# Narrow matmul groups for layer 2's values and scores, a new place for its values in the time slot, and small VectorE instructions rewritten or moved to ScalarE

## The chip, the cores and the metric

The kernel runs on one core of a Trainium2 chip. The metric is the device time of one execution in microseconds (us), which is slightly longer than the span that the profile covers. The core's engines work in parallel, each through its own list of instructions in a fixed order: TensorE (PE, with its weight loads shown apart as PEld), VectorE (DVE), ScalarE (ACT), GpSimd (POOL) and SyncE (SP, which here issues every transfer). They wait for each other by semaphores. Matmul results land in PSUM and are carried from there to SBUF by DVE or ACT.

## What is computed

Four attention layers follow each other on x (4 images of 1024 rows and 256 columns). Layers 0 and 1 fill the first 1713 us and are touched only in one side job. Layer 2 is cross attention of 16 heads of width 16 to a context of 77 rows, with a factor for each score and a mask:

```python
scores = jnp.einsum('bhqd,bhkd->bhqk', q, k) / jnp.sqrt(jnp.float32(d))
scores = scores * attention_weights
scores = jnp.where(attention_mask, -jnp.inf, scores)
p_attn = jax.nn.softmax(scores, axis=-1)
out = jnp.einsum('bhqk,bhkd->bhqd', p_attn, v)
...
x = queries + out          # after out @ Wo.T + bo
return (x - mu) * jax.lax.rsqrt(var + LN_EPS) * gamma + beta
```

Layer 3 is a cross attention of 16 heads of width 64 to the same 77 context rows, after an RMS norm. All is float32.

## The kernel before

**Stages.** Layers 0 and 1 run over image and group of four heads, with a planner (`step`, `Job`) that puts side jobs between bursts of score matmuls. A side job has a share of the step in which its pieces are due; `values2` (layer 2's values of the context) and `keys2` are such jobs in layer 0. The values go to DRAM tensors and come back when layer 2 begins.

**Layers 2 and 3** run in time slots, one per tile of 128 rows (32 tiles, i = 0 to 31). `slot23` writes the order of the work in a slot by hand. A tile's layer 2 is spread over six slots: scores (`score2`) and maxima in slot i, exponentials (`exps2`), sums (`sums_of`, tile `den2`) and division (`divided`, POOL) in i+1, transposition (`turned_into`, tile `pT2`) in i+3, values (`values_of2`) in i+4, output (`out2`, `add2`) in i+5. Layer 3 of a tile starts 12 slots later (`LAG`): scores and their exponential (`score3`, `exp3`), in the next slot sums and division, in the one after it transposition (`pT3`) and output (`out3`). So slots 0 to 11 hold layer 2 alone, 12 to 36 both, 37 to 45 layer 3 alone. A middle slot has one tile of each stage. On PE its order is: transposition for layer 3, `score2`, `out3`, `values_of2`, `score3`, transposition for layer 2, `out2`.

**Between the layers** `between(g)` works on four tiles at a time: mean and variance (`stats4` on DVE, the power on POOL, L293), normalising on ACT (L1502), gamma and beta on POOL, statistics again, scaling by the inverse RMS (`normed`, L316, tile `xn`, four instructions on DVE), and transposition into `xT3` (`turned_x`, two DVE instructions, L1442). Its pieces are taken up at the four calls of `more()` in a slot, two pieces a call. `prep2(b)` (the queries of an image) is taken up in the same way, in two slots of an image.

**PSUM.** Pair tiles of two banks (`big`, 2 buffers) hold scores; the pool `sm` has 3 buffers that every transposition, `pvT` and projection takes in turn, so each new one waits until the third before it has been read out; the pool `pv` has one, for `po2` and `po3`.

**Scores of layer 2 before.** The keys stand in `kb` four times, each time with only every fourth head's rows kept. A matmul takes 64 rows (4 heads) and 4 x 77 columns; there are two such per pair tile and two pair tiles. Every float32 matmul other than a transposition shows as two instructions in the profile.

**Values of layer 2 before.** The 1232 columns (16 heads x 77) of the transposed weights fill 10 chunks of 128 rows. The values stand in DRAM as a block diagonal matrix, 128 output columns wide, loaded with five transfers per image (`loads2`), and `values_of2` multiplies chunk by chunk: 11 matmuls of 128 x 128 on 128 columns.

**Maxima.** L1558 bounds the 16 maxima of each row and scales them, in one DVE instruction on 128 x 16.

Of the kernel before, what the change touches and what calls it, by code (L numbers as in the profile page):

```python
# [31 lines left out]
def tile_xattn_seq(ctx: ExitStack, tc: tile.TileContext, d: dict, out: bass.AP):  # L32
# [902 lines left out]
    HALF, DIAG = HH * S * P, S * P + DH  # L935
    kept_v = dram.tile([NB, 2, HH * DIAG], F32, name="kept_v")
    stg = wpool.tile([P, 1024], F32, name="stg", tag="s7")
    turn = [0]

# [25 lines left out]

    def values2():

        n = NB * 2 * HH * DIAG // P // 8
        nc.gpsimd.memset(stg[:, 0:n], 0.0)
        nc.sync.dma_start(  # L970
            out=kept_v.rearrange("b e x -> (b e x)").rearrange("(p k n) -> p k n", p=P, n=n),
            in_=stg[:, 0:n].unsqueeze(1).to_broadcast([P, 8, n]),
        )
        yield
        for b in range(NB):
            pk = sm.tile([S, D], F32, name="pk", tag="sm")
            for c in range(2):
                mm(pk, ctxT[:, b, c, :], l2["Wv"][:, c, :], start=(c == 0), stop=(c == 1))
            v = place(3, NS)[:S, 0:D]
            nc.vector.tensor_tensor(v, pk, rows["bv2"][:S], ALU.add)  # L980
            for e in range(2):
                to = kept_v[b, e].rearrange("(j x) -> j x", x=DIAG)[:, 0 : S * P]
                nc.sync.dma_start(
                    out=to.rearrange("j (s p) -> s j p", p=P)[:, :, 0:DH],
                    in_=v[:, P * e : P * e + P].rearrange("s (j r) -> s j r", r=DH),
                )
            yield

    def keys2():
# [419 lines left out]

    def loads2(b):  # L1410

        V = late.tile([P, NC + 1, P], F32, name="V2", tag="V2", bufs=2)
        lo, hi = [kept_v[b, e, 0:HALF].rearrange("(r n) -> r n", n=P) for e in range(2)]

        k = HH * S % P
        nc.gpsimd.memset(V[:, 4:6, :], 0.0)
        nc.sync.dma_start(
            out=V[:, 0:4, :], in_=lo[0 : 4 * P].rearrange("(c p) n -> p c n", p=P)
        )
        nc.sync.dma_start(out=V[0:k, 4, :], in_=lo[4 * P :])  # L1420
        nc.sync.dma_start(out=V[k:P, 5, :], in_=hi[0 : P - k])
        nc.sync.dma_start(
            out=V[:, 6:10, :], in_=hi[P - k : 5 * P - k].rearrange("(c p) n -> p c n", p=P)
        )
        nc.sync.dma_start(out=V[0:HSIZE, 10, :], in_=hi[5 * P - k :])
        shared["v2", b] = V
        yield

    def half_rows(e):
        return slice(64 * e, 64 * e + 64)  # L1430

    def turned_x(dst, rows, g):

        for c in range(2):
            pt = sm.tile([P, 4, P], F32, name="ptx", tag="sm")
            for i in range(4):
                nc.tensor.transpose(pt[:, i, :], rows[i][:, c * P : (c + 1) * P], ident)
            src = pt.rearrange("p i n -> p (i n)")
            if g is None:
                nc.scalar.copy(dst[:, c, :], src)  # L1440
            else:
                nc.vector.tensor_scalar(dst[:, c, :], src, g[:, c : c + 1], None, ALU.mult)  # L1442
            yield

    def prep2(b):
# [42 lines left out]
    def between(g):  # L1488

        b, t0 = divmod(4 * g, NT)  # L1490
        x = xs[b]
        st = small.tile([P, 4, 6], F32, name="st4", tag="st6")
        mv = small.tile([P, 4, 2], F32, name="mv4", tag="mv", bufs=3)
        rs = small.tile([P, 4], F32, name="rs4", tag="rs", bufs=3)
        yield from stats4(st, mv, rs, g, 1e-5, False)
        away = late.tile([P, 4], F32, name="away", tag="away")
        nc.gpsimd.tensor_tensor(away, mv[:, :, 0], rs, ALU.mult)
        nc.gpsimd.tensor_scalar(away, away, -1.0, None, ALU.mult)
        yield True
        for k in range(4):  # L1500
            xt = x[:, t0 + k, :]
            nc.scalar.activation(  # L1502
                xt, xt, AF.Identity, bias=away[:, k : k + 1], scale=rs[:, k : k + 1]
            )
            nc.gpsimd.tensor_tensor(xt, xt, rows["gamma"], ALU.mult)
            nc.gpsimd.tensor_tensor(xt, xt, rows["beta"], ALU.add)
            yield k == 3
        st = small.tile([P, 4, 6], F32, name="st4", tag="st6")
        mv = small.tile([P, 4, 2], F32, name="mv4", tag="mv", bufs=3)
        rs = small.tile([P, 4], F32, name="rs4", tag="rs", bufs=3)  # L1510
        yield from stats4(st, mv, rs, g, 1e-6, True)
        xn = []
        for k in range(4):
            xt = small.tile([P, D], F32, name="xn", tag="xn", bufs=4)
            normed(xt, x[:, t0 + k, :], None, rs, k)
            xn.append(xt)
            if k % 2:
                yield k == 3
        yield True
        xT = shared["xT3"][:, g % 2]  # L1520
        yield from turned_x(xT, xn, cols["L3_xattn_norm_w"])
        shared["ready3"] = g

    LAG = 12

    def score2(a, i):

        b, t = a["b"], a["t"]
        qT, kb = shared["b2", b], shared["k2"]
        assert shared["ready2"] >= b  # L1530
        fs, mk = shared.pop(("side", i))
        if i + 1 < NB * NT:
            load_sides(i + 1)
        s = a["s"] = new_scores("s2", 4)
        for o in range(2):
            ps = pair_tile()
            for e in range(2):
                r = half_rows(e)
                mm(
                    ps[:, e, 0 : 4 * S].rearrange("p (h s) -> p h s", s=S),  # L1540
                    qT[r, o, P * t : P * t + P],
                    kb[r, o, :, b, :],
                )
            so = slice(o * HH * S, (o + 1) * HH * S)
            nc.vector.tensor_tensor(
                s[:, so].rearrange("p (i n) -> p i n", i=2), ps[:, :, 0 : 4 * S],
                fs[:, so].rearrange("p (i n) -> p i n", i=2), ALU.mult,
            )
        sv = s[:, 0:HK]
        nc.vector.copy_predicated(sv, mk, low.to_broadcast([P, HK]))  # L1550

    def maxima2(a):
        nm = a["nm"] = late.tile([P, H], F32, name="nm", tag="m16")
        nc.vector.tensor_reduce(
            nm, a["s"][:, 0:HK].rearrange("p (h k) -> p h k", k=S), axis=AX.X, op=ALU.max
        )

        nc.vector.tensor_scalar(nm, nm, 0.1 * NEG, -SC, ALU.max, ALU.mult)  # L1558

    def exps2(a, heads):  # L1560
        for h in heads:
# [22 lines left out]
    def values_of2(a):  # L1584

        V = shared["v2", a["b"]]
        pv = sm.tile([P, 2, P], F32, name="pvT", tag="sm")
        for k in range(NC + 1):
            o, c = (0, k) if k < 5 else (1, k - 1)
            r = slice(0, rows_in(c))  # L1590
            mm(pv[:, o, :], V[r, k, :], a["pT"][r, c, :], start=k in (0, 5), stop=k in (4, NC))
        oT = a["oT"] = late.tile([P, 2, P], F32, name="oT", tag="oT", bufs=2)
        nc.scalar.copy(oT, pv)

# [50 lines left out]
    def slot23(i, two, three, more):  # L1645
# [29 lines left out]
        elif i < n + 5:  # L1675
# [9 lines left out]
            if p1:  # L1685
                exps2(p1, range(4, 8))
            more()
            if c2:
                out3(c2)
            if p1:  # L1690
                exps2(p1, range(8, 12))
            if a:
                maxima2(a)
            if p4:
                values_of2(p4)
            more()
            if p1:
                exps2(p1, range(12, H))
            if c:
                score3(c, j)  # L1700
            more()
            if p3:
                turned_into(p3, "pT2")
            if c:
                exp3(c)
            if p1:
                sums_of(p1, "den2")
            if p5:
                out2(p5)
                add2(p5)  # L1710
            more()
            if p1:
                divided(p1)
# [36 lines left out]
    def jobs0(b, quad):  # L1750
# [142 lines left out]
    late = ctx.enter_context(tc.tile_pool(name="late", bufs=2))  # L1893
    kb = shared["k2"] = late.tile([P, 2, 4, NB, S], F32, name="kb", tag="kb", bufs=1)
    nc.sync.dma_start(out=kb.rearrange("p o h b s -> p o h (b s)"), in_=kept_k)
    load_sides(0)
    run(loads2(0))
    run(prep2(0))
# [65 lines left out]
```

## Time and profile before

| | us |
|---|---|
| median of 3 runs (2308.59 to 2311.46) | 2310.94 |
| the profiled execution, whole | 2310.56 |
| its span in the profile | 2308.8 |
| PE busy / DVE busy / ACT busy / POOL busy | 2158.3 / 1506.8 / 1027.5 / 652.2 |
| first load of layer 2's stage issued | 1713.2 |
| last layer 2 score tile masked (slot 31) | 2140.8 |

The span is 1.76 us shorter than the execution's time, and that execution is 0.38 us faster than the median. Busy shares over the whole span mix four layers, so everything that follows is read from the window of 1713 to 2309 us. PE's "busy" counts a matmul from its start to a modelled end; starts of consecutive matmul groups show better where PE was held up.

### The profile page before, as it was taken

To read this page: it belongs to the slowest core of one execution; us is meant where nothing else is said; L and a number is where in the kernel's file an instruction comes from. 1 tells how busy PE (TensorE), PEld (TensorE's weight loads), DVE (VectorE), ACT (ScalarE), POOL (GpSimd) and SP (SyncE) were. 2 spreads that over 40 slices of the span, in tenths; PEclk is the share of its full clock that TensorE was granted. 3 is DMA by queue.
4 is the path that set the end of the run, shared out by engine and by line. 5 is a ranking of instruction groups with operands and counts; after the bars stand their busy time and mean duration, and the time that the engine had idled before them with its cause. 6 is when DMAs were issued, how large, how long until landed. Compare 5 with 4: busy or idle time off the path is not lost.

```text
span 2308.8 us, 41140 instructions
## 1 busy us (share of the span) xinstructions
PE 2158.3 (93%) x16842; PEld 1358.9 (59%) x16874; DVE 1506.8 (65%) x2476; ACT 1027.5 (45%) x1716; POOL 652.2 (28%) x959
## 2 busy tenths in 40 slices
PE   4999999999999999999989999999988899999999
PEld 2544444555555455554556665666656678788877
DVE  3756567755566455754375666777748888788654
ACT  1144444434444444344533444544547655555322
POOL 2011113111131112310152233333333444444432
PEclk9899999999999999999989999999999999999999
DMA  7221121100000000101000010111025412313000
GB/s 217 55 57 68 31 65 41 40 6 15 7 15 2 10 11 6 38 1 19 6 15 6 15 26 16 21 20 20 15 74 152 136 51 68 100 49 95 10 10 17
DMA packets 87858, 93.98 MB, mean 41 GB/s; under 512 B 35714, under 2 KB 77558, under 8 KB 87542
## 3 DMA queue, kind: packets, MB, share of 16 engines
q1 hardware_dynamic: 87670, 91.35, 15.2%
q8 instruction: 133, 2.18, 0.4%
q14 instruction: 55, 0.45, 0.1%
HBM read 55.31 MB, written 18.39 MB: 32 GB/s over the span
## 4 chain that ended last, share of the span: by engine, by line
PE 67%; DVE 15%; ACT 4%; issue 2%; POOL 2%; DMA 0%; DVEq 0%; ACTq 0%; POOLq 0%; SPq 0%
PE ps L51 26%; PE po L51 12%; PE pv L51 6%; PE pp L51 5%; PE ph L51 4%; DVE mpart L672 3%; PE pvT L51 2%; DVE ms L1138 2%; PE ppv L51 2%; PE psT L1375 2%; PE pvw L51 1%; DVE mrow L1142 1%; PE pm L590 1%; PE pt L607 1%; ACT pe L738 1%
## 5 line engine op out<-in xcount | busy, mean ns | idle before, releaser
L51 PE MATMUL ps<-qk 32*128 32x192 f32 (+9 forms) x6528 | 581.8, 428 | 57.9 <-DVE mpart L672 25.1
L738 ACT ACTIVATE pe<-ps 128x1024 f32<-128x1024 f32 (+2 forms) x384 | 363.3, 952 | 589.5 <-PE ps L51 579.9
L51 PEld LDWEIGHTS ps<-qk 32*128 32x128 f32 (+1 forms) x6528 | 315.8, 185 | 295.6 <-issue 75.3
L672 DVE TENSOR_REDUCE mpart<-ps 128x2 f32<-128x1024 f32 (+4 forms) x384 | 331.0, 885 | 241.6 <-PE ps L51 240.8
L741 POOL TENSOR_SCALAR_AFFINE_SELECT pe<-pe 128x256 f32<-128x256 f32 (+1 forms) x192 | 95.2, 497 | 665.3 <-ACT pe L738 664.3
L1214 ACT ACTIVATE pew<-ps 128x768 f32<-128x768 f32 x128 | 103.4, 812 | 196.4 <-PE ps L51 196.4
L1574 POOL TENSOR_TENSOR s<-s,den 128x1232 f32<-128x1232 f32 x64 | 144.2, 2254 | 130.2 <-DVE den L1570 125.2
L1219 POOL TENSOR_SCALAR_AFFINE_SELECT pew<-pew 128x512 f32<-128x512 f32 x128 | 81.9, 640 | 337.7 <-ACT pew L1214 337.6
L1138 DVE TENSOR_TENSOR ms<-ps,maskw 128x768 f32<-128x768 f32 x128 | 122.1, 954 | 69.6 <-PE ps L51 68.1
L51 PE MATMUL po<-U,pT 128*128 128x256 f32 (+1 forms) x640 | 147.2, 385 | 10.8 <-DVE x L1602 7.6
L51 PE MATMUL pv<-pe,va 128*32 128x512 f32 (+3 forms) x1536 | 157.1, 496 | 0.0
L51 PE MATMUL ph<-yT,w 128*128 128x256 f32 x512 | 143.1, 401 | 2.4 <-DVE va L401 1.0
L51 PEld LDWEIGHTS po<-U,pT 128*128 128x128 f32 (+1 forms) x640 | 120.3, 192 | 35.0 <-ACT pT L1376 19.6
L51 PEld LDWEIGHTS po<-w,hT 128*128 128x128 f32 x800 | 111.8, 193 | 47.7 <-issue 38.9
L51 PE MATMUL ps<-G,xT 128*128 128x308 f32 x512 | 139.2, 422 | 0.0
L51 PE MATMUL po<-w,hT 128*128 128x128 f32 (+1 forms) x800 | 138.1, 317 | 0.9 <-ACT hT L904 0.9
L1563 ACT ACTIVATE s<-s,nm 128x77 f32<-128x77 f32 x512 | 134.8, 358 | 5.9 <-DVE nm L1558 5.9
L1376 ACT COPY pT<-psT 128x512 f32<-128x512 f32 (+1 forms) x192 | 87.7, 522 | 105.8 <-PE psT L1375 105.2
L665 DVE TENSOR_REDUCE mpart<-ps 128x8 f32<-128x1024 f32 x64 | 78.2, 1225 | 82.6 <-PE ps L51 80.0
L51 PEld LDWEIGHTS ph<-yT,w 128*128 128x128 f32 x512 | 88.8, 192 | 64.0 <-issue 50.8
L1142 DVE TENSOR_REDUCE mrow<-ms 128x4 f32<-128x768 f32 x128 | 122.2, 955 | 4.4
L51 PEld LDWEIGHTS ps<-G,xT 128*128 128x128 f32 x512 | 94.3, 190 | 30.1
(202 smaller groups left out, 3297.6 us busy)
## 6 DMA issues: line engine op xcount, KB each, us to landing
side<-in_fside_t SPq DMA_DIRECT2D x32, 616.0 KB
qk<-st SPq DMA_DIRECT2D x256, 64.0 KB
side<-in_mask_t SPq DMA_DIRECT2D x32, 154.0 KB
G<-kept_g SPq DMA_DIRECT2D x4, 1232.0 KB
U<-kept_u SPq DMA_DIRECT2D x4, 1152.0 KB
x<-in_x SPq DMA_DIRECT2D x8, 512.0 KB
out<-x SPq DMA_DIRECT2D x32, 128.0 KB
kept_g<-st SPq DMA_DIRECT2D x22, 154.0 KB
```

What stands on the lines that cost most here:

```text
L51: nc.tensor.matmul(o, lhsT, rhs, start=start, stop=stop, **kw)
L665: nc.vector.tensor_reduce(mpart[self.own][:, :, 2 * p : 2 * p + 2, 0].rearrange("p t j -> p j t"), ps.rearrange("p j (t n) -> p j t n", n= ...
L672: nc.vector.tensor_reduce(mpart[bl][:, i, 2 * p : 2 * p + 2, ci], ps[:, :, o : o + w], axis=AX.X, op=ALU.max,)
L738: nc.scalar.activation(pp[:n, :, o:512], ps[:n, :, o:512], AF.Exp, scale=SC)
L741: nc.gpsimd.affine_select(out=own, in_=own, compare_op=ALU.is_ge, fill=0.0, base=0, pattern=[[0, 2], [0, k], [1, P]], channel_multiplier=-1,)
L1138: nc.vector.tensor_tensor(v, ps.rearrange("p j (i n) -> p j i n", i=2)[:, :, :, 0:n], (maskw[:, 1:2] if w else maskw).unsqueeze(1).to_broa ...
L1142: nc.vector.tensor_reduce(mo, v, axis=AX.X, op=ALU.max, negate=True)
L1214: nc.scalar.activation(pp[:, :, :, 0 : P + WIN], ps.rearrange("p j (i n) -> p j i n", i=2)[:, :, :, 0 : P + WIN], AF.Exp, scale=SC,)
L1219: nc.gpsimd.affine_select(out=pf[:, :, 0:P], in_=pf[:, :, 0:P], compare_op=ALU.is_ge, fill=0.0, base=0, pattern=[[0, 4], [1, P]], channel_ ...
L1376: nc.scalar.copy(pT[:, 4 * group : 4 * group + n, :], ps[:, 0:n, :])
L1563: nc.scalar.activation(hs, hs, AF.Exp, bias=a["nm"][:, h : h + 1], scale=SC)
L1574: nc.gpsimd.tensor_tensor(s3, s3, a["den"].unsqueeze(2).to_broadcast([P, H, S]), ALU.mult)
```

## The change

*Values.* They are written to a DRAM tensor `kept_w` in rows of 32 (a pair of heads, each in its half of the row). A new side job `spread2`, taken up in layer 0 while image 2 is worked on, copies them from DRAM to DRAM into `kept_v`, with 17 transfers: `CUTS` holds the 17 pieces into which 8 head pairs (154 rows each) and 10 chunks of 128 rows cut each other. An image's values then come with one transfer. `values_of2` has 17 matmuls with 128 x 32 weights; the four head pairs of a half write 32 output rows each, in turn.

*Scores.* `score2` has 8 matmuls, each with 32 rows (2 heads) and 2 x 77 columns. The four row groups write to four PSUM banks, so both pair tiles are filled before the first is read out, and each of the two DVE instructions that reads them (L1545 before) takes half of the columns of both halves.

*Small instructions.* L1558 becomes two `tensor_tensor` with a tile `bound` of two columns; `xn` and `xT3` are made by ACT.

*Order.* In a slot of both layers `values_of2` comes before `out3`, and `out2` and `add2` before the transposition for layer 2.

```diff
+    PAIR = 2 * S
+    CUTS = [
+        (c, q, max(P * c, PAIR * q), min(P * c + P, PAIR * q + PAIR))
+        for q in range(HH) for c in range(PAIR * q // P, (PAIR * q + PAIR - 1) // P + 1)
+    ]
+    kept_w = dram.tile([NB, HK, HP], F32, name="kept_w")
+    kept_v = dram.tile([NB, P, len(CUTS), HP], F32, name="kept_v")
...
+    def spread2():
+        for k, (c, q, lo, hi) in enumerate(CUTS):
+            nc.sync.dma_start(
+                out=kept_v[:, lo - P * c : hi - P * c, k, :], in_=kept_w[:, lo:hi, :]
+            )
+            yield
...
-        V = late.tile([P, NC + 1, P], F32, name="V2", tag="V2", bufs=2)
...
+        V = late.tile([P, len(CUTS), HP], F32, name="V2", tag="V2", bufs=2)
+        nc.sync.dma_start(out=V, in_=kept_v[b])
...
-                nc.vector.tensor_scalar(dst[:, c, :], src, g[:, c : c + 1], None, ALU.mult)
+                nc.scalar.activation(dst[:, c, :], src, AF.Copy, scale=g[:, c : c + 1])
...
-            normed(xt, x[:, t0 + k, :], None, rs, k)
+            nc.scalar.activation(xt, x[:, t0 + k, :], AF.Copy, scale=rs[:, k : k + 1])
...
+        pair = [pair_tile() for _ in range(2)]
         for o in range(2):
-            ps = pair_tile()
-            for e in range(2):
-                r = half_rows(e)
+            for g in range(4):
+                e = 2 * (g % 2)
                 mm(
...
+                    qT[rows_of(g), o, P * t : P * t + P], kb[rows_of(g), o, e : e + 2, b, :],
+                    skip_group_check=True,
                 )
...
-        nc.vector.tensor_scalar(nm, nm, 0.1 * NEG, -SC, ALU.max, ALU.mult)
+        nc.vector.tensor_tensor(nm, nm, bound[:, 0:1].to_broadcast([P, H]), ALU.max)
+        nc.vector.tensor_tensor(nm, nm, bound[:, 1:2].to_broadcast([P, H]), ALU.mult)
...
-        for k in range(NC + 1):
-            o, c = (0, k) if k < 5 else (1, k - 1)
-            r = slice(0, rows_in(c))
-            mm(pv[:, o, :], V[r, k, :], a["pT"][r, c, :], start=k in (0, 5), stop=k in (4, NC))
+        for o in range(2):
+            own = [
+                [(k, c) for k, (c, q, _, _) in enumerate(CUTS) if q == 4 * o + j] for j in range(4)
+            ]
+            for n in range(max(map(len, own))):
+                for j in range(4):
+                    if n < len(own[j]):
+                        k, c = own[j][n]
+                        mm(
+                            pv[rows_of(j), o, :], V[:, k, :], a["pT"][:, c, :],
+                            start=(n == 0), stop=(n == len(own[j]) - 1), skip_group_check=True,
+                        )
...
             more()
+            if p4:
+                values_of2(p4)
             if c2:
                 out3(c2)
...
             if a:
                 maxima2(a)
-            if p4:
-                values_of2(p4)
             more()
...
             if c:
                 score3(c, j)
             more()
+            if p5:
+                out2(p5)
+                add2(p5)
             if p3:
                 turned_into(p3, "pT2")
...
-            if p5:
-                out2(p5)
-                add2(p5)
             more()
...
+        if b == 2:
+            j.append(Job(keep("sp2", spread2), 5, 0.3, 0.9))
```

More of the change, by code (lines that the diff above doesn't have):

```diff
@@ L933, in tile_xattn_seq @@
     kept_u = dram.tile([NB, H, S, D], F32, name="kept_u")
-    HALF, DIAG = HH * S * P, S * P + DH
-    kept_v = dram.tile([NB, 2, HH * DIAG], F32, name="kept_v")
+    PAIR = 2 * S
[5 more added lines that the diff above has]
+    kept_v = dram.tile([NB, P, len(CUTS), HP], F32, name="kept_v")
     stg = wpool.tile([P, 1024], F32, name="stg", tag="s7")
@@ L966, in values2 @@
     def values2():
-        n = NB * 2 * HH * DIAG // P // 8
+        n = len(CUTS) * HP
         nc.gpsimd.memset(stg[:, 0:n], 0.0)
         nc.sync.dma_start(
-            out=kept_v.rearrange("b e x -> (b e x)").rearrange("(p k n) -> p k n", p=P, n=n),
-            in_=stg[:, 0:n].unsqueeze(1).to_broadcast([P, 8, n]),
+            out=kept_v.rearrange("b p k n -> p b (k n)"),
+            in_=stg[:, 0:n].unsqueeze(1).to_broadcast([P, NB, n]),
+        )
+        nc.sync.dma_start(
+            out=kept_w.rearrange("b (s q) n -> s b (q n)", s=S),
+            in_=stg[:S, 0 : H * HP].unsqueeze(1).to_broadcast([S, NB, H * HP]),
         )
@@ L981, in values2 @@
             for e in range(2):
-                to = kept_v[b, e].rearrange("(j x) -> j x", x=DIAG)[:, 0 : S * P]
                 nc.sync.dma_start(
-                    out=to.rearrange("j (s p) -> s j p", p=P)[:, :, 0:DH],
-                    in_=v[:, P * e : P * e + P].rearrange("s (j r) -> s j r", r=DH),
-                )
+                    out=kept_w[b].rearrange("(q e s) n -> e s q n", e=2, s=S)[e, :, :, DH * e : DH * e + DH],
+                    in_=v.rearrange("s (q e r) -> s q e r", e=2, r=DH)[:, :, e, :],
+                )
+            yield
+    def spread2():
+        for k, (c, q, lo, hi) in enumerate(CUTS):
+            nc.sync.dma_start(
+                out=kept_v[:, lo - P * c : hi - P * c, k, :], in_=kept_w[:, lo:hi, :]
+            )
             yield
@@ L1410, in loads2 @@
     def loads2(b):
-        V = late.tile([P, NC + 1, P], F32, name="V2", tag="V2", bufs=2)
[L1413 to L1425, printed above, removed]
+        V = late.tile([P, len(CUTS), HP], F32, name="V2", tag="V2", bufs=2)
+        nc.sync.dma_start(out=V, in_=kept_v[b])
         shared["v2", b] = V
@@ L1534, in score2, with of_pair @@
         s = a["s"] = new_scores("s2", 4)
+        pair = [pair_tile() for _ in range(2)]
         for o in range(2):
-            ps = pair_tile()
-            for e in range(2):
-                r = half_rows(e)
-                mm(
-                    ps[:, e, 0 : 4 * S].rearrange("p (h s) -> p h s", s=S),
-                    qT[r, o, P * t : P * t + P],
-                    kb[r, o, :, b, :],
-                )
-            so = slice(o * HH * S, (o + 1) * HH * S)
+            for g in range(4):
+                e = 2 * (g % 2)
+                mm(
+                    pair[g // 2][:, g % 2, PAIR * o : PAIR * o + PAIR].rearrange(
+                        "p (h s) -> p h s", s=S
+                    ),
+                    qT[rows_of(g), o, P * t : P * t + P], kb[rows_of(g), o, e : e + 2, b, :],
+                    skip_group_check=True,
+                )
+        def of_pair(v, k):
+            v = v[:, 0:HK].rearrange("p (o g n) -> p g o n", o=2, g=4)
+            return v[:, 2 * k : 2 * k + 2]
+        for k in range(2):
             nc.vector.tensor_tensor(
-                s[:, so].rearrange("p (i n) -> p i n", i=2), ps[:, :, 0 : 4 * S],
-                fs[:, so].rearrange("p (i n) -> p i n", i=2), ALU.mult,
+                of_pair(s, k),
+                pair[k][:, :, 0 : 2 * PAIR].rearrange("p i (o n) -> p i o n", o=2),
+                of_pair(fs, k), ALU.mult,
             )
@@ L1587, in values_of2 @@
         pv = sm.tile([P, 2, P], F32, name="pvT", tag="sm")
-        for k in range(NC + 1):
-            o, c = (0, k) if k < 5 else (1, k - 1)
-            r = slice(0, rows_in(c))
-            mm(pv[:, o, :], V[r, k, :], a["pT"][r, c, :], start=k in (0, 5), stop=k in (4, NC))
+        for o in range(2):
[9 more added lines that the diff above has]
+                            start=(n == 0), stop=(n == len(own[j]) - 1), skip_group_check=True,
+                        )
         oT = a["oT"] = late.tile([P, 2, P], F32, name="oT", tag="oT", bufs=2)
@@ L1895, in tile_xattn_seq @@
     nc.sync.dma_start(out=kb.rearrange("p o h b s -> p o h (b s)"), in_=kept_k)
+    bound = late.tile([P, 2], F32, name="bound", tag="bound", bufs=1)
+    nc.gpsimd.memset(bound[:, 0:1], 0.1 * NEG)
+    nc.gpsimd.memset(bound[:, 1:2], -SC)
     load_sides(0)
```

## The prediction

> **What bounds the kernel now.** The page's busy shares say PE (93%), but over four layers. I read windows of the last stage first: PE, PEld, DVE, ACT and POOL busy, with counts, then the granted clock and the DMA share.
>
> ```profile
> 1770.00:1800.00 30.00, 27.14 (x190) 21.54 (x188) 26.16 (x38) 24.22 (x82) 11.19 (x11) 1.00 0.44 145
> 1900.00:1950.00 50.00, 49.28 (x294) 41.20 (x294) 45.49 (x69) 27.00 (x79) 25.20 (x31) 1.00 0.15 46
> 2200.00:2250.00 50.00, 47.24 (x234) 38.27 (x233) 28.21 (x53) 13.56 (x24) 20.11 (x28) 1.00 0.03 11
> ```
>
> With both layers in a slot (second row) PE is full and DVE is at 91%; ACT has half its time free. With layer 2 alone (first row) the chain of waits runs along DVE: the masking L1550 starts at 1781.39, 1788.02 and 1794.66, a slot of 6.63 us that DVE's own instructions fill. DMA is idle enough everywhere. So what PE saves counts only in slots 12 to 36. Next, the timeline of PE in such a slot:
>
> ```profile
> 1887.61 4.56 PE L51 MATMUL po<-U,pT 128*128 128x256 f32 x20 [0.79 <-DVE x L1602]
> 1892.00 2.62 PE L51 MATMUL pvT<-pT,V 128*128 128x128 f32 x22
> 1894.46 4.31 PE L51 MATMUL ps<-G,xT 128*128 128x308 f32 x16
> 1898.61 1.25 PE L1375 MATMUL psT<-ident,s 128*128 128x128 f32 x10
> 1899.70 1.03 PE L51 MATMUL po<-w2q,oT 128*128 128x256 f32 x4
> 1900.56 1.25 PE L1375 MATMUL psT<-ident,s 128*128 128x128 f32 x10
> 1901.75 1.31 PE L51 MATMUL ps<-kb,qT 64*128 64x308 f32 x8
> 1902.99 4.59 PE L51 MATMUL po<-U,pT 128*128 128x256 f32 x20
> ```
>
> From start to start: out3 4.39, layer 2's values 2.46, layer 3's scores 4.15, transposition 1.09, out2 0.86, transposition 1.19, layer 2's scores 1.24: 15.38 us and no gap. Four slots, one turn of `between`, take 64.17 (out3 starts at 1854.52 and 1918.69): 15.97, 17.12 (with 0.87 of xn's transpositions), 15.38, 15.70. The gaps in three of them are 0.2 to 0.8.
>
> Then ACT in the same slot, since PE's new order leans on it:
>
> ```profile
> 1899.30 1.35 ACT L1376 COPY pT<-psT 128x512 f32<-128x512 f32 x3 [3.27 <-PE psT L1375]
> 1900.54 1.24 ACT L1643 ACTIVATE s<-s 128x1232 f32<-128x1232 f32 x1
> 1901.67 1.34 ACT L1376 COPY pT<-psT 128x512 f32<-128x512 f32 x3
> ```
>
> This chain decides: from the start of layer 2's transposition (1898.61) the copies, layer 3's exponential and the first copy for layer 3 (0.59) take until 1902.26, 3.65 us and 0.04 to reach PE: 3.69. Before, out3 asked for that copy at 1902.99, so ACT had 0.7 us to spare.
>
> **The change, part by part.** "Turn" is the time from the end of layer 3's scores on PE to the next such end.
>
> *Narrow values.* Out go 11 matmuls (22 instructions, 2.46 us), in come 17 (34 instructions). The nearest rows are layer 1's 32-column matmuls, taken in turn over four column groups, and for the scores its 32-row ones:
>
> ```profile
> 1405.65 0.86 PE L51 MATMUL pvw<-pew,va 128*32 128x192 f32 x16
> 1406.43 1.99 PE L51 MATMUL po<-wout,cT 128*128 128x256 f32 x8
> 1409.39 0.75 PE L51 MATMUL pvw<-pew,va 128*32 128x192 f32 x16
> 1410.07 0.66 PE L590 MATMUL pm<-ident,mrow 128*128 128x128 f32 x4
> ...
> 1417.25 0.93 PE L51 MATMUL ps<-qk 32*128 32x192 f32 x16
> 1418.11 1.12 PE L51 MATMUL pp<-xT,w1q 128*128 128x512 f32 x2
> ```
>
> 16 instructions take 0.68 (half of them on 128 columns) to 0.78, that is 42 to 49 ns each against 112 ns for a full one. 32 in turn at 42 make 1.36, the last cut of the fifth head pair stands alone (two at about 0.1): 1.55 us. Ends: 1.25 (32 at 33 ns, the rest as before) and 2.07 (34 at 61 ns, the mean busy time of the 128x192 group, 45.5 us for 768). I take 1.55, from the nearest row.
>
> [...]
>
> *Narrow scores.* 16 instructions on 154 columns for 8 on 308: at 0.86 for 16 on 192 columns, 0.85 at most instead of 1.24. Lower end 0.69 (16 at 43 ns).
>
> *The new order and who waits.* `pvT` takes the `sm` buffer that layer 3's first transposition group used, so the values now wait for that group's copy; and out2 stands ahead of layer 2's transposition, which pushes the copies, exponential and next copies by 0.86. Values start 0.86 + 3.69 = 4.55 us after layer 3's scores; PE itself would be ready after 0.86 + 1.09 + 1.19 + 0.85 = 3.99. Half a microsecond of PE is idle: the narrow scores save nothing in a plain slot. Plain turn: 4.55 + 1.55 + 4.40 + 4.15 = 14.65, against 15.38.
>
> *Work given to ACT.* Per four tiles four scalings leave DVE and join ACT's queue between layer 3's exponential and its copies, at the end of a slot. There they wait for the power on POOL:
>
> ```profile
> 1869.43 1.04 POOL L293 TENSOR_TENSOR rs<-rs,nhalf 128x4 f32<-128x4 f32 x1
> ...
> 1917.08 1.08 ACT L1502 ACTIVATE x<-x,away,rs 128x256 f32<-128x256 f32 x2
> ...
> 2176.73 2.07 ACT L1502 ACTIVATE x<-x,away,rs 128x256 f32<-128x256 f32 x4
> ```
>
> POOL's power ended at 1870.47, 4.92 us after layer 3's scores (1865.55). In the new order out3 ends just before layer 3's scores, and DVE's add after it, the maxima and two statistics come before the first reduction of these scores; that pushes DVE by 0.5. So: 5.45, four scalings like L1502 2.07, first copy and hop 0.63: values start at 8.15. Queued behind the waiting scaling are the three copies for layer 3 and the exponentials; behind the copies, values and out3. This turn is 8.15 + 10.10 = 18.25. Ends: 14.65 if POOL's result always comes early, 19.3 with a microsecond more. I take the chain, whose links are all in rows. In the turn in which ACT has two L1502 there (0.99 from start to the next copy) values start at 5.54: 15.64. The two xT3 copies fall where ACT is free (about 0.6 each).
>
> Four turns: 14.65 + 15.64 + 18.25 + 14.65 + 0.87 = 64.06 against 64.17. Five rounds: **-0.5 us**. DVE's stalls of 0.5 and 0.8 on L1602 are gone; the scaling's wait on ACT takes their place.
>
> *Slots with `prep2`* (two each for images 2 and 3). Its projections keep PE busy while ACT catches up (before, 8.56 us from 1963.43 to 1971.99), so values and scores both count: 0.91 + 0.39 = 1.30 in one, 1.02 in the other, where I counted 0.73 and 0.06 above: **-3.1**.
>
> *Slots 32 to 36*, no layer 2 scores: before, out3 started 3.69 after layer 3's scores; now values at 4.55. Even, but for one slot with xn's transpositions ahead (12.3 to 11.5 from score end to score start): **-1.0**.
>
> *Slots 0 to 11.* DVE paces them. L1558 becomes two instructions, of about 0.18 each:
>
> ```profile
> L1558 DVE TENSOR_SCALAR nm<-nm x32: 174/176/978, 1729.9 to 2145.6; 128x16 f32<-128x16 f32 x32
> ```
>
> +0.18 in about 8 slots, +1.4. Between 1754 and 1772 PE is on the chain: one values group and two scores, -1.7. At 1814 DVE no longer scales (2.42 us on the chain): the exponentials now wait behind the scalings on ACT, which gives part back: -1.9. Together **-2.2**.
>
> L1558's maximum is a wait while POOL reads. [...] The mean of L1558 is 422 ns, so that is 0.25 us in 32 tiles, 8 us of DVE, none of them on a chain counted here.
>
> *DMA.* `spread2`: 17 issues of about 0.33 us on SP in image 2 of layer 0, ahead of some `qk` transfers. SP waits for PE 649 us in all, and PE waited for a `qk` transfer 3.2 us in the first 200: 0, ends 0 and +6. Clearing 1704 KB rather than 2468 at 45 us, one V transfer for five, no clearing of V by POOL (0.31 on the chain at 1713): -0.3. The tail after slot 37: +0.3.
>
> Sum: -0.5 - 3.1 - 1.0 - 2.2 - 0.3 + 0.3 = -6.8, so a profiled execution of 2303.8. The median stood 0.38 above that execution: **2304.2 us**. Values count in some 25 slots: the ends of their price give -7.5 and +13.
>
> **Rivals.**
> *PE paces the middle* (the scaling never waits: DVE, 8 us per four slots lighter, runs ahead). The third turn falls to 14.65: -3.6 x 5 = -18, 2286. For: DVE loses 4 x 0.76 and 2 x 0.74 per group. Against: the statistics stand in DVE's queue behind the reductions of layer 3's scores, so they can't run ahead of PE.
> *Slower: the narrow matmuls don't overlap.* Place: values, 25 slots; at 61 ns an instruction 2.07, +13, 2317; at 109 ns (mean of a 32-column weight load) 3.7, +54. It is slower than before by over 0.2% from 2.0 us on (59 ns). For: 17 pieces of 128 columns are shorter than any row but a few. Against: 42 to 49 ns measured on 192.
> *Nothing* (the wait one microsecond longer five times, L1545's new pattern a little slower): 2309 to 2311.
>
> **Chances.** Forecast 0.50, by itself 2298 to 2310; PE paces 0.17; narrow matmuls slow 0.17; nothing 0.16. About 0.2% (4.6 us) is what can be told from no change. Faster: 0.17 and 0.8 of the forecast, 0.57. Same: the rest of the forecast, most of the last, 0.24. Slower 0.19. Range 2287 to 2318: the PE rival's time and the 61 ns case.
>
> **What would show it.** Right: values x34 with 1.4 to 1.7 from start to next start; a wait of about 0.5 on ACT's pT copy before values, 3.5 to 4 in every fourth slot, where ACT waits for POOL; no L316 and no wait for L1602 on PE; DVE waiting for out3's end. Wrong: values above 2 us, or ACT finding POOL's result ready, or PE waiting for something not named here, above all a DMA in layer 0.

## The result, and the profile after

The changed kernel takes **2312.45 us** (median; 2310.99 to 2316.55), the kernel before 2308.53 in the same comparison (2302.87 to 2312.80). The ratio is 1.0017, with a 95% interval of 1.0011 to 1.0024: slightly slower, less than the 0.2% that the prediction called telling, and 8.2 us above the forecast of 2304.2. The profiled execution took 2312.34 us, with a span of 2310.6 (2310.56 and 2308.8 before).

The same three windows as before, with the busy time of PE, PEld, DVE, ACT and POOL, then the granted clock and the DMA share:

```profile
1770.00:1800.00 30.00, 22.50 (x278) 15.73 (x276) 25.82 (x36) 23.64 (x82) 11.49 (x11) 0.94 0.31 97
1900.00:1950.00 50.00, 43.82 (x335) 35.59 (x335) 39.22 (x64) 28.89 (x82) 25.08 (x31) 0.93 0.18 56
2200.00:2250.00 50.00, 46.07 (x246) 36.49 (x246) 25.30 (x47) 15.77 (x29) 19.75 (x26) 1.00 0.03 11
```

The second row is the one to read. PE was busy for 49.28 of 50 us before and is busy for 43.82 now, and no other engine is full. The saving on PE is there, but it has become idle time, and the granted clock has fallen from 1.00 to 0.93. PE's timeline shows a plain turn first:

```profile
1900.61 1.03 PE L51 MATMUL po<-w2q,oT 128*128 128x256 f32 x4
1901.47 1.26 PE L1391 MATMUL psT<-ident,s 128*128 128x128 f32 x10
1902.89 1.28 PE L1391 MATMUL psT<-ident,s 128*128 128x128 f32 x10 [0.17 <-ACT pT L1392]
1904.11 0.81 PE L51 MATMUL ps<-kb,qT 32*128 32x154 f32 x16
1905.17 1.28 PE L51 MATMUL pvT<-pT,V 128*32 128x128 f32 x34 [0.26 <-ACT pT L1392]
1906.38 4.59 PE L51 MATMUL po<-U,pT 128*128 128x256 f32 x20
1910.80 4.31 PE L51 MATMUL ps<-G,xT 128*128 128x308 f32 x16
```

Values start 4.56 us after layer 3's scores and take 1.21 from start to next start. The turn is 14.34 us (1900.61 to 1914.95), against 15.38 before. Then the turn in which ACT scales `xn`, on PE, ACT and POOL, with two windows of it:

```profile
1867.90 0.81 PE L51 MATMUL ps<-kb,qT 32*128 32x154 f32 x16
1872.66 2.34 PE L51 MATMUL pvT<-pT,V 128*32 128x128 f32 x34 [3.95 <-ACT pT L1392]
1874.93 6.48 PE L51 MATMUL po<-U,pT 128*128 128x256 f32 x20
...
1867.35 1.23 ACT L1664 ACTIVATE s<-s 128x1232 f32<-128x1232 f32 x1
1870.43 1.71 ACT L1519 ACTIVATE xn<-x,rs 128x256 f32<-128x256 f32 x4 [1.85 <-POOL rs L293]
1872.05 1.31 ACT L1392 COPY pT<-psT 128x512 f32<-128x512 f32 x3
...
1869.36 1.04 POOL L293 TENSOR_TENSOR rs<-rs,nhalf 128x4 f32<-128x4 f32 x1
...
1872.00:1877.00 5.00, 4.34 (x39) 3.42 (x40) 3.13 (x3) 4.63 (x17) 3.08 (x3) 0.50 0.00 0
1877.00:1882.00 5.00, 5.00 (x24) 4.28 (x23) 0.56 (x2) 0.12 (x1) 0.63 (x2) 0.82 0.00 0
```

ACT waits for POOL's power and then scales; layer 3's copies stand behind that, and PE idles for 3.95 us (3.95 again in the third such turn, 4.2 in the other three). All of this had been forecast. The last two rows had not: after the idle time the granted clock is 0.50 for 5 us and 0.82 for the next 5, so that the 34 narrow matmuls take 2.27 us instead of 1.21 and out3 6.31 instead of 4.42.

Where the time went, by stages. A turn here ends where a group of layer 3's scores ends in PE's timeline (start plus duration; the first such group is number 0). The first row is counted from the start of the span, and each column adds up to its span.

| stage, us | before | after | after - before |
|---|---|---|---|
| to layer 2's first mask (L1550, now L1562) | 1726.79 | 1726.07 | -0.7 |
| to the end of scores 2 | 138.92 | 138.50 | -0.4 |
| scores 2 to 19 | 282.05 | 289.31 | +7.3 |
| scores 19 to 23 | 63.98 | 58.25 | -5.7 |
| scores 23 to the end | 97.06 | 98.47 | +1.4 |

The third stage holds five turns with the scaling. From one score end to the next they take 21.86, 21.49, 20.54, 20.78 and 20.80 us, against 16.81 or 16.82 before.

### The profile page after: what moved, and what is told of

Same layout as the page of the kernel before. It is cut to its first block, busy times and chain, and to the rows that moved or that the text cites. A ratio compares the mean times of both kernels' runs of the same rounds, so it can differ in the third digit from the quotient of the medians.

```text
span 2310.6 us, 42496 instructions
## 1 busy us (share of the span) xinstructions
PE 2127.1 (92%) x17514; PEld 1317.2 (57%) x17514; DVE 1476.3 (64%) x2460; ACT 1047.6 (45%) x1764; POOL 650.8 (28%) x957
## 3 DMA queue, kind: packets, MB, share of 16 engines
q8 instruction: 138, 2.26, 0.4%
## 4 chain that ended last, share of the span: by engine, by line
PE 67%; DVE 14%; ACT 7%; issue 2%; POOL 2%; DVEq 0%; ACTq 0%; POOLq 0%
PE ps L51 25%; PE po L51 13%; PE pv L51 6%; PE pp L51 6%; PE ph L51 4%; DVE mpart L672 3%; DVE ms L1154 2%; PE ppv L51 2%; PE pvT L51 2%; ACT pT L1392 1%; PE pvw L51 1%; DVE mrow L1158 1%; PE pt L607 1%; PE pm L590 1%; ACT pe L738 1%
```

## The experiments

Theory A: the scaling's wait costs twice, as idle time of PE and as a lower clock after it, and the rest of the change gains. Its rivals: the narrow matmuls are slow by themselves; the new order is what costs, or what is needed; VectorE's small pair costs; DVE takes over as the bound once PE is let go. All edits are to the changed kernel. A ratio is always to the kernel before, on the same chip.

**The scaling back on DVE.**

```diff
-            nc.scalar.activation(xt, x[:, t0 + k, :], AF.Copy, scale=rs[:, k : k + 1])
+            normed(xt, x[:, t0 + k, :], None, rs, k)
```

> The changed kernel with one part undone: the four scalings between the layers (tile xn) are VectorE's again. Theory A (the scalings stand in ScalarE's queue ahead of layer 3's copies and wait there for GpSimd's power; values wait for the copies; TensorE idles about 4 us, after which its granted clock is low): the turn with the scalings falls from 21.0 us to 16 to 17 (VectorE's own lag is what is left), five times, so 2288 to 2293. Theory B (VectorE would pace the middle anyway, so ScalarE's wait costs nothing by itself): 2308 to 2313, with VectorE's scalings in the place of the wait.

Measured: 2299.33 us (2293.92 to 2300.42), ratio 0.9949 [0.9930, 0.9968]. The scaling turn goes as Theory A says: values start 4.70 us after layer 3's scores and take 1.21 to next start, and the turn is 15.36 us. But the gain is 6 us short of its forecast. The turn after it shows why, on PE:

```profile
1887.06 0.79 PE L51 MATMUL ps<-kb,qT 32*128 32x154 f32 x12 [0.92 <-DVE s L1648]
1888.86 1.28 PE L51 MATMUL pvT<-pT,V 128*32 128x128 f32 x34 [1.00 <-ACT pT L1392]
```

DVE, with four scalings more, is late with layer 3's subtraction (L1648), and the lag reaches PE one turn later: 16.5 us instead of 14.3. In two of the five rounds values were slow there too, 2.26 and 1.66 us busy instead of 1.28 (turns of 19.1 instead of 15.4, 18.2 instead of 14.3).

**The scaling one call of the work between tiles later.** It still runs on ACT and still needs POOL's power, but stands behind layer 3's copies and the first exponentials of the next slot, and not ahead of them.

```diff
+        yield True
         xn = []
         for k in range(4):
...
                 yield k == 3
-        yield True
         xT = shared["xT3"][:, g % 2]
```

> The changed kernel with the scalings still on ScalarE, but taken up one call later, behind layer 3's copies and the first eight exponentials of the next slot, when GpSimd's power is long there. Theory A: no wait ahead of the copies, values 4.6 us after layer 3's scores in this turn as in the plain ones, no fall of the clock: 21.0 to 14.4 plus a little, 2279 to 2285. Theory B: 2308 to 2313. Theory C (the narrow matmuls, not the idle time, lower the granted clock): the wait goes but values and layer 3's output stay slow in this turn, 2290 to 2295.

Measured: **2277.22 us** (2276.53 to 2283.37), ratio 0.9867 [0.9846, 0.9888], a little better than the theory's range. PE's timeline in the same turn, then a window:

```profile
1862.26 1.28 PE L51 MATMUL pvT<-pT,V 128*32 128x128 f32 x34 [0.40 <-ACT pT L1392]
1863.47 4.59 PE L51 MATMUL po<-U,pT 128*128 128x256 f32 x20
...
1860.00:1900.00 40.00, 38.75 (x318) 31.73 (x318) 35.63 (x54) 25.94 (x77) 17.68 (x18) 1.00 0.17 53
```

3.95 us of idle time became 0.40, the clock is 1.00, and the scaling turns take 15.36 to 15.61. Against the changed kernel the third stage lost 27.9 us (289.31 to 261.39). Another 5.2 lie ahead of it: from layer 2's first mask to the end of scores 0 it takes 101.70 us instead of 106.86, because the scaling of the first group of tiles, for which ACT waited 3.84 us for POOL's power (at 1815.53) with exponentials behind it, is out of the way too. One misplaced wait had cost more than everything else gained.

**Matmuls in the idle time.** To part the clock from the wait, PE gets work to do while ACT waits: 8 spare matmuls into a tile that nobody reads; the wait stays.

```diff
+            if c and i % 4 == 3 and i < 32:
+                spare = pvp.tile([P, D], F32, name="spare", tag="pv")
+                for k in range(8):
+                    mm(spare, l2["Wo"][:, 0, 0:P], l2["Wo"][:, 1, :])
             if p4:
                 values_of2(p4)
```

> The changed kernel with ScalarE's wait kept and TensorE's idle time in it filled: eight extra 128 x 128 x 256 matmuls into a PSUM tile that nobody reads, between layer 2's scores and values, in the five slots of that turn. They are extra work of about 3.4 us each time, in an idle time of 3.95. Theory A: values and layer 3's output fall back from 2.2 and 5.2 to 6.3 us to 1.2 and 4.4, the clock stays at 1.00 there, and the kernel gets 8 to 13 us faster for doing more: 2299 to 2304. Theory C: the two stay slow, 2312 or above.

Measured: 2303.25 us (2300.81 to 2306.33), ratio 0.9981 [0.9968, 0.9993]. PE's timeline in the scaling turn, then the window that answers to the one at 0.50:

```profile
1872.83 3.72 PE L51 MATMUL spare<-w2q 128*128 128x256 f32 x16
1876.73 1.28 PE L51 MATMUL pvT<-pT,V 128*32 128x128 f32 x34 [0.18 <-ACT pT L1392]
1877.94 4.59 PE L51 MATMUL po<-U,pT 128*128 128x256 f32 x20
...
1872.00:1877.00 5.00, 4.76 (x45) 3.76 (x48) 4.79 (x8) 3.15 (x7) 4.21 (x6) 1.00 0.01 3
```

Values start as late as before, 8.26 us after the scores, but at full clock. The five scaling turns take 18.91, 19.15, 18.90, 19.15 and 19.16 us: together 95.3 instead of 105.5. So 10.2 us of the changed kernel are the lower clock alone. That narrow matmuls are slow by themselves falls with this: 34 of them take 1.20 to 1.21 us from start to next start in this run, in the scaling turns as in the others.

**How much idle time it takes.** 4 and 2 spare matmuls instead of 8.

> The changed kernel with 4 spare matmuls on 128 by 256 (instead of 8, into a tile that nobody reads) between layer 2's scores and its values in every fourth slot: TensorE still idles some 2.1 us of the 4. Theory A (the clock falls with the length of the idle time, and 2.0 us lowered it once in the kernel before): it falls in some of the five turns and not in others, values 1.21 or 2.3, out3 4.4 or above 5: 2304 to 2312. Rival (any idle time of the wait lowers it): in all five, 2311 to 2314.

> The changed kernel with 2 spare matmuls there: TensorE idles about 3 us. Theory A: the clock falls in all or nearly all five turns: 2309 to 2314. Rival (only about 4 us of idle time lower it): out3 at 4.4 in most turns, 2303 to 2307.

Measured, one execution each: 2304.23 and 2311.53 us. The first two rows are PE's timeline with 4 spare matmuls, the last two with 2:

```profile
1874.80 1.28 PE L51 MATMUL pvT<-pT,V 128*32 128x128 f32 x34 [1.90 <-ACT pT L1392]
1876.01 4.59 PE L51 MATMUL po<-U,pT 128*128 128x256 f32 x20
```

```profile
1872.34 2.34 PE L51 MATMUL pvT<-pT,V 128*32 128x128 f32 x34 [2.77 <-ACT pT L1392]
1874.61 6.51 PE L51 MATMUL po<-U,pT 128*128 128x256 f32 x20
```

With 1.90 us idle the five turns are those with the wait filled (18.90 to 19.14), with 2.77 those of the changed kernel (21.90, 20.84, 20.55, 20.80, 20.79). The granted clock was 1.00 from 1872 to 1880 us with 4 spare matmuls, and 0.50 from 1872 to 1878 with 2. I had expected a mixture at 1.90; there is none. Half of the filling does all that the whole does, a quarter does nothing. Length isn't the whole rule: with the narrow matmuls alone (below) 2.68 us of idle time left out3 at 4.56, while a wait of 1.21 was once followed by an out3 of 6.24.

The clock records in the traces of the kernel before and of the changed kernel show what else counts. In each of the two the granted clock changes only at moments that lie a whole number of 3.41 us apart, on a grid whose place differs between them: 2152.83 us is such a moment before, 1871.96 in the changed kernel. Take the windows of these grids from 1836 to 2235 us, and PE's idle share by its modelled busy time. From 1.00 the clock fell after all 6 windows in which PE idled for 59% or more, and after none of the 218 with 46% or less. It rose again after the 6 windows at 0.50 in which PE was busy throughout, and after neither of the other two (79% and 43% busy). The first four rows are such windows of the changed kernel, around the wait of 3.95 us shown above; the last two are those of the narrow matmuls alone into which the 2.68 us fell:

```profile
1868.54:1871.96 3.42, 0.17 (x8) 0.00 (x0) 3.25 (x6) 1.57 (x5) 3.17 (x6) 1.00 0.00 0
1871.96:1875.37 3.41, 2.71 (x35) 2.15 (x36) 3.17 (x3) 3.41 (x13) 1.49 (x3) 0.50 0.00 0
1875.37:1878.79 3.42, 3.42 (x9) 2.70 (x9) 0.00 (x0) 1.26 (x5) 2.26 (x2) 0.50 0.00 0
1878.79:1882.20 3.41, 3.41 (x21) 3.05 (x21) 0.76 (x2) 0.32 (x1) 0.00 (x0) 1.00 0.00 0
...
2133.89:2137.30 3.41, 1.92 (x14) 1.54 (x12) 3.34 (x5) 1.19 (x3) 0.00 (x0) 1.00 0.00 0
2137.30:2140.71 3.41, 2.22 (x10) 2.01 (x11) 2.60 (x5) 3.41 (x12) 2.29 (x2) 1.00 0.00 0
```

PE idled for 95% of the first window, and the clock fell at its end. The second window was only 79% busy, so a third one at 0.50 followed. The 2.68 us were shared by two windows, 44% and 35% idle, and the clock stayed at 1.00. The 1.21 us lay with a gap of 0.22 in a window that was 42% idle, counted back from these rows, and out3 was slow all the same: the share is not the whole rule either. A gap of 1.90 us fills 56% of a window of 3.41 at most. One of 2.77 us could be shared by two windows as well; by this estimate the turns were slow five times of five because of where the grid stood in that run, and would not be after every gap of this length.

**The old places of values and out2**, all else as changed: values behind the maxima, out2 behind the sums.

```diff
             more()
-            if p4:
-                values_of2(p4)
             if c2:
                 out3(c2)
...
             if a:
                 maxima2(a)
+            if p4:
+                values_of2(p4)
...
-            if p5:
-                out2(p5)
-                add2(p5)
             if p3:
                 turned_into(p3, "pT2")
...
+            if p5:
+                out2(p5)
+                add2(p5)
```

> The changed kernel with the order in a slot of before: layer 3's output ahead of layer 2's values, layer 2's transposition ahead of its output. All else as changed. Theory A: the third turn keeps its wait (layer 3's output needs the same copies), the plain turns lose the 0.43 us that values wait: about -0.4 in 15 turns, 2304 to 2309. Rival (the new order is what the narrow values need): 2315 to 2320.

Measured: 2302.35 us (2301.81 to 2307.88), ratio 0.9977 [0.9961, 0.9993], below both forecasts. The order is not what the narrow matmuls need: the plain turn is 13.86 us (1883.53 to 1897.39), half a microsecond shorter. The scaling's wait is there all the same and now meets out3, which takes 6.27 us behind it instead of 4.58:

```profile
1871.04 6.27 PE L51 MATMUL po<-U,pT 128*128 128x256 f32 x20 [3.29 <-ACT pT L1392]
```

**Old places and the later scaling together.**

> The kernel with the scalings one call later (2277), with values and out2 in their places of before. Theory A (the new order costs, since it puts values behind ScalarE's copy): plain turns of 13.9 instead of 14.35 us, 0.5 less in some 20 slots: 2265 to 2271. Rival (the new order is worth having once nothing else waits, since out3 then has its copy early; in the old one out3 waits for it): 2277 to 2285, with TensorE waiting before out3 in most turns.

Measured: 2273.94 us (2272.24 to 2275.45), ratio 0.9848 [0.9828, 0.9868], between the two forecasts. Plain turns are again 13.86, but in one turn of four out3 waits 1.07 to 1.41 us for DVE's `x` (L1623), the stall that the kernel before had, and in another 1.19 for ACT's copy. They take back more than half of the gain that was hoped for.

**The narrow matmuls alone**: old places, the scalings and scaled copies on DVE, one small instruction.

> Only layer 2's narrow values and scores, with their data path, are kept of the change: values and out2 stand in their old places, the scalings and the scaled copies are on VectorE and the small pair is one instruction, as before. Theory A (the narrow matmuls are worth what their rows say, 1.25 + 0.43 us a turn, and the rest of the change lost it): TensorE no longer waits for a scaling on ScalarE, turns of 13.9 to 15 us against 15.4 before, limited by VectorE's lag in one of four: 2282 to 2296. Rival (VectorE, 91% busy before, paces at once without the work given to ScalarE, so that narrow matmuls alone gain nothing): 2302 to 2309.

Measured: 2291.73 us (2290.13 to 2295.70), ratio 0.9929 [0.9912, 0.9946], in Theory A's range. PE's part of the change is worth some 16 us by this ratio; the rest of the change took that away. DVE's lag limits it: in the middle PE waits 8.6 us in all for L1622 (L1623 of the changed kernel).

**The small pair as one instruction again.**

```diff
-        nc.vector.tensor_tensor(nm, nm, bound[:, 0:1].to_broadcast([P, H]), ALU.max)
-        nc.vector.tensor_tensor(nm, nm, bound[:, 1:2].to_broadcast([P, H]), ALU.mult)
+        nc.vector.tensor_scalar(nm, nm, 0.1 * NEG, -SC, ALU.max, ALU.mult)
```

> The changed kernel with one thing undone: the two small instructions L1570 and L1571 are the one two-scalar instruction of before again. Theory A (the clock falls behind the scaling's wait; the pair costs its own time where layer 2 runs alone and VectorE paces): each of these 8 or so slots is 0.2 us shorter (7.05 to 6.85), nothing else moves on the chain: 2309 to 2312. Rival (the pair is worth having, since the single one waits while GpSimd reads, up to 978 ns in the profile before): nothing gained in the slots alone, some of the single ones 0.5 us longer in slots on the chain: 2312 to 2318.

Measured: 2305.18 us (2303.41 to 2309.61), ratio 0.9985 [0.9973, 0.9997], a gain of some 7 us against the changed kernel, where 2 had been expected, and below both forecasts. Two reasons stand in the trace. Where layer 2 runs alone, the slot falls from 7.05 to 6.83 us, as expected. And the pair was on the chain of the scaling's wait. DVE in the changed kernel, in the slot shown above, with POOL reading beside it:

```profile
1862.26 0.17 DVE L1570 TENSOR_TENSOR nm<-nm,bound 128x16 f32<-128x16 f32 x1
1862.47 0.71 DVE L1571 TENSOR_TENSOR nm<-nm,bound 128x16 f32<-128x16 f32 x1
1863.10 0.41 DVE L1486 BATCH_NORM_STATS2 st<-x 128x6 f32<-128x256 f32 x1
...
1861.61 0.73 POOL L1509 TENSOR_TENSOR x<-x,r_gamma 128x256 f32<-128x256 f32 x1
1862.42 0.73 POOL L1510 TENSOR_TENSOR x<-x,r_beta 128x256 f32<-128x256 f32 x1
```

From the pair's start to the statistics 0.84 us pass, where the single instruction took 0.08 in this place. The statistics feed POOL's power, which ends 6.00 us after layer 3's scores with the pair and 5.23 without it, and PE's wait goes from 3.95 to 3.18. These two account for the profiled executions' 2.7 us (2312.34 to 2309.61, and this kernel's first mask came 1.3 us later). The median lies 4.4 us lower than that execution, and this part is open: eight of the twelve executions took 2303.4 to 2305.7 us, four 2308.8 to 2309.6, and only one of the four left a trace. The recorded mean clock was 0.978 in the eight and 0.975 to 0.977 in the four, so the clock's falls may account for it; that isn't shown.

**All of ACT's work out of the way.** The two normalising activations (L1506) one call later as well, out2 behind layer 2's transposition, the single small instruction.

```diff
         yield True
+        yield True
         for k in range(4):
             xt = x[:, t0 + k, :]
...
-        yield True
         xT = shared["xT3"][:, g % 2]
...
+            if p3:
+                turned_into(p3, "pT2")
             if p5:
                 out2(p5)
                 add2(p5)
-            if p3:
-                turned_into(p3, "pT2")
```

> The kernel with the scalings one call later (2277), in which the two normalising activations are one call later as well, out2 stands behind layer 2's transposition, and the small pair is one instruction again. Theory A (ScalarE's queue ahead of the values is all that still holds TensorE in the turns): the 1.23 us wait in one turn of four goes, 5 times 1.0; the 0.26 wait in the others goes, 5 to 7; VectorE's small instruction 2: 2264 to 2270. Rival (VectorE, 12.8 us busy of 14.35, takes over as soon as TensorE is let go): 2272 to 2278, with waits for VectorE's s or x on TensorE.

Measured: 2267.26 us (2265.93 to 2267.63), ratio 0.9819 [0.9799, 0.9838]: Theory A's range, and DVE does not take over. Two waits were new: values waited 2.44 us once after layer 2's last scores, and a transposition 2.92 us for `xn` in the tail. So the later normalising was kept only for the first six groups of four tiles (`if g < 6`; the scalings keep their later place in all).

> The kernel with normalising and scalings one call later, out2 behind layer 2's transposition and the single small instruction (2267), but the last two groups of four tiles are normalised where the changed kernel has it. Theory A (there the later normalising only collided: values waited 2.44 us once in slots 32 to 36 and layer 3's transpositions 2.92 us in the tail): both waits go, 4 to 7 us less: 2260 to 2263. Rival (they come from the two layer 3 groups' order, not from the later call): 2266 to 2268.

Measured: **2259.79 us** (2259.06 to 2260.43), ratio 0.9779 [0.9764, 0.9793], the best of all, 51 us below the kernel before and at the lower end of Theory A's forecast. The window of the middle:

```profile
1900.00:1950.00 50.00, 49.73 (x380) 39.84 (x377) 42.06 (x60) 33.88 (x91) 25.97 (x33) 1.00 0.20 69
```

PE is full again, and a plain turn takes 13.66 us, where it took 15.38 before and 14.34 in the changed kernel.

**The same (2259.79 us) with the old places.**

> The same as the run named e9_later_but_last, but with values and out2 in their places of before. Theory A (with ScalarE's queue clear the old places let TensorE go on without a wait, and 0.26 us a turn less is lost; VectorE's x then ends the idle time once in four turns, as 1.4 us in the earlier run with old places): about the same, 2258 to 2266. Rival (the old places are better by half a microsecond a turn): 2250 to 2257.

Measured: 2269.47 us (2268.22 to 2273.36), ratio 0.9825 [0.9808, 0.9841]: 10 us worse than with the new place of values, outside both forecasts. Four turns take 57.51 us instead of 55.84. One of the four holds a wait on DVE's `x` (L1625 here):

```profile
1864.38 4.56 PE L51 MATMUL po<-U,pT 128*128 128x256 f32 x20 [1.00 <-DVE x L1625]
```

And the plain turn is 13.86 us, not 13.66, without any wait. The rows of that turn, first from the changed kernel with the old places (2302.35 us, where it takes 13.86 as well) and then from the one with the new place (2259.79 us), show where:

```profile
1886.68 0.81 PE L51 MATMUL ps<-kb,qT 32*128 32x154 f32 x16
1887.42 4.58 PE L51 MATMUL po<-U,pT 128*128 128x256 f32 x20
1891.93 1.28 PE L51 MATMUL pvT<-pT,V 128*32 128x128 f32 x34
1893.14 4.41 PE L51 MATMUL ps<-G,xT 128*128 128x308 f32 x16
1897.39 1.25 PE L1391 MATMUL psT<-ident,s 128*128 128x128 f32 x10
```

```profile
1875.94 0.81 PE L51 MATMUL ps<-kb,qT 32*128 32x154 f32 x16
1876.68 1.28 PE L51 MATMUL pvT<-pT,V 128*32 128x128 f32 x34
1877.89 4.59 PE L51 MATMUL po<-U,pT 128*128 128x256 f32 x20
1882.31 4.31 PE L51 MATMUL ps<-G,xT 128*128 128x308 f32 x16
1886.46 1.25 PE L1391 MATMUL psT<-ident,s 128*128 128x128 f32 x10
```

In the old places narrow and full matmuls alternate, and each of the two full groups is 0.1 us longer: out3 takes 4.51 from start to next start instead of 4.42, layer 3's scores 4.25 instead of 4.15. The new place puts the two narrow groups side by side. Standing behind narrow matmuls isn't by itself what costs 0.1 us, since out3 stands behind them in both orders; what does is not shown. So what the order is worth depends on the rest: it cost some 9 us in the changed kernel, and is worth 10 here, where less of ACT's work stands ahead of the values and out2 stands one place later than in the change; no run parts these two.

## Why the prediction was wrong, by its own steps

The step that failed is "This turn is 8.15 + 10.10 = 18.25". The 8.15 was nearly right: values start 8.26 to 8.50 us after layer 3's scores. The 10.10 took values, out3 and scores at full clock, after 4 us in which PE does nothing. With xn's transpositions (0.87) the step says 19.12; at full clock, with filled idle time, the turns are 18.90 to 19.16, and in the changed kernel they average 21.09. That is 5 x 1.97 = 9.9 us, more than the whole miss of 8.2. The kernel that keeps the wait and loses only the clock's fall takes 2303.25, within a microsecond of the forecast. That it comes so near is partly luck: by the table, the change gained 4.7 us more than forecast between scores 19 and 23, and some 3.3 less from the first mask to the end of scores 2. The profile of before held the warning. PE's timeline and a window there:

```profile
2152.84 6.24 PE L51 MATMUL po<-U,pT 128*128 128x256 f32 x20 [2.03 <-DVE x L1602]
...
2152.00:2156.00 4.00, 3.16 (x8) 2.56 (x9) 2.25 (x5) 4.00 (x16) 3.23 (x3) 0.60 0.00 0
```

The same out3 takes 4.39 elsewhere; here, after 2.03 us of idle time, it took 6.24 at a clock of 0.60. The sum had no term for it, nor had any rival.

- *Narrow values*: 1.21 us, not 1.55, and just under the lower end (1.25); 36 ns an instruction. (The 61 ns of the upper end is a slip: 45.5 us for 768 are 59.) The rival in which they don't overlap is refuted. Behind narrow matmuls out3 takes 4.42 from start to next start in the changed kernel, against 4.39 before; 0.1 more than that shows in the old places alone (4.51).
- *Narrow scores*: 0.81 busy, as said, and as said worth nothing in a plain slot.
- *The new order*: right link by link. Values start 4.56 after the scores (4.55 forecast), 5.53 in the turn with two normalising activations (5.54); the turns are 14.34 and 15.31 instead of 14.65 and 15.64, shorter by what values were overpriced. Four whole rounds still lost 1.68, 0.62, 0.37 and 0.61 us against before, more than all of it in the scaling turn.
- *Work given to ACT*: the chain was named rightly, its links were not all. Four scalings took 1.71, not 2.07, and POOL's power ended 6.00 after the scores, not 5.45; the two cancelled. The second is the small pair. The prediction read a wait "while POOL reads" off the one instruction that it replaces, 978 ns at most, and saw none of that "on a chain counted here". The pair waits too, and on this chain: L1571 took 0.71 us with POOL's L1509 and L1510 running all the while, against 0.17 with POOL idle.
- *Slots with* `prep2`: 2.53 us saved in the second pair of such turns (39.02 to 36.49), 1.84 in the first (33.48 to 31.64); 2.32 each had been forecast.
- *Slots 32 to 36*: -5.7 instead of -1.0. The turn of 17.92 us before, which held the 2.03 us wait and the slow out3 just shown, is 14.34 now. The prediction priced neither.
- *Slots 0 to 11*: -1.3 from the first mask to the twelfth, instead of -2.2, but +1.4 from the first mask to the end of scores 0 (105.44 to 106.86). Behind the twelfth, the exponentials wait behind the first group's scaling, which the prediction named as what "gives part back"; with the scaling one call later the stretch takes 101.70, so this wait takes back 5.2 us, more than all that was saved there. The slot that DVE paces grew by 0.42, not by 0.18. The pair is half of it; the other half is the multiplication of layer 2's scores with its new pattern, whose price was taken as nothing. DVE before and after:

```profile
1779.91 1.44 DVE L1545 TENSOR_TENSOR s<-ps,side 128x616 f32<-128x616 f32 x2
```

```profile
1780.22 1.64 DVE L1556 TENSOR_TENSOR s<-ps,side 128x616 f32<-128x616 f32 x2
```

- *DMA*: the start of layer 2 moved by -0.7 us, but over all these runs it lies anywhere from 1724.4 to 1730.0, so that neither the -0.3 nor a loss can be told. The 17 issues took 0.56 to 1.15 us each, 0.71 on average, not 0.33.
- *The tail*: +1.4 instead of +0.3; the last scaling on ACT holds up its transpositions (1.89 us instead of 1.33) and the scores behind them.
- *The rival "PE paces"*: a scaling that no longer holds up PE came as soon as it was moved (2277, below the rival's 2286), but not by DVE running ahead. DVE is 4.4 us lighter per four slots there (56.81 us busy in the third round before, 52.41 after), which is what the terms behind "For" add up to, not 8. The prediction's reason against it, that the statistics can't run ahead, was right for the code as it stood.

## What to carry to other kernels

Idle time of the engine that bounds a kernel can cost more than its length: here gaps of about 4 us cost 1.6 to 2.9 us more each by the lower clock behind them. Look in the profile for the same matmul group after a gap, and compare its time and the granted clock with the undisturbed one. Before work is given to an engine with half its time free, read what stands behind it in that engine's queue and when its input is ready; an engine with much free time is still the wrong place for an instruction that waits, and moving it one step down the queue was worth 35 us here. When a change with several parts comes out even, run the parts alone: here one of them was worth 16 us, and one wait hid it.

## What the runs showed of the hardware that was not expected

- PE's clock fell to 0.50 after gaps far shorter than I would have thought: one of 2.03 us in the kernel before (0.50 from 2152.83 to 2156.24 us). In the traces before and after, from 1836 to 2235 us, it fell with how much of a window of the 3.41 us grid PE idled, as the rows of such windows above show, and the window did not have to be idle as a whole: 59% and 66% were enough, once each. In layers 0 and 1 of the same two traces less could do, 30 to 40% in 10 of 33 windows at 1.00, so PE's busy share is not all that counts.
- A fallen clock stayed down for whole windows: 6.83 us in the first two of the changed kernel's five turns (1871.96 to 1878.79 in the first), 3.41 in the other three. Against the turns with filled idle time that cost 2.9 and 2.3 us, and 1.6 each. So in these runs the price went by where the grid stood, and not by whether the gap was 2.8 or 4.0 us long.
- 34 narrow matmuls on four column groups in turn took 36 ns each on 128 columns, less than layer 1's 42 to 49 on 192.
